# Neighbourhood attention with a mixture of experts on one core: the order of two products, and the layout of the transposed bias rows

## The chip, the cores and the metric

The kernel runs on one core of a Trainium2 chip. The metric is the device time of one execution in microseconds. Before the change it was run three times (median 4380.1 us, 4376.23 to 4390.58). One further execution was recorded by the hardware profiler; all lines of profiles come from such an execution, and line numbers (L445) are those of the kernel.

## The reference

Input x is 2 x 128 x 256 x 256 (batch, channels, rows, columns), all in float32. The output is two residual steps:

```python
x = x + conv(_ln_c(x), W_qkv, W_out, rel_height, rel_width)   # attention
t = _to_tokens(x)
t = t + ffn(_ln_t(t), router_w, router_b, expert_w, expert_b) # top-2 of 8 experts
```

The attention works on windows of 8 x 8 queries and 12 x 12 keys around them, with 4 heads of 32 channels:

```python
q = q * SCALE
attn = jnp.einsum('bnd,bmd->bnm', q, k)
attn = attn + rel_pos_emb(q, rel_height, rel_width) + FIXED_MASK
attn = jax.nn.softmax(attn, axis=-1)
out = jnp.einsum('bnm,bmd->bnd', attn, v)
```

`FIXED_MASK` is minus infinity wherever the row or the column distance is odd in its table, so that a query only meets keys of its own row and column parity. `rel_pos_emb` adds to a score a term that depends on the query and the row distance, and one on the query and the column distance. The second step gives each token to the two experts with the highest router probability, weighted.

## The kernel before, in words

The image is cut into strips of 8 rows, 32 a batch item, 64 in all. Because of the mask, a strip falls apart into four independent planes (two row parities by two column parities), each of 4 x 128 pixels. The main loop (L809) makes one turn for each of the 256 planes, and seven more for what is left of the experts. In one turn, `n`, it does the attention of plane n, the projections of plane n + 1, and one piece of 512 tokens of the normalisation, the routing and the experts of earlier rows. Everything of the loop stands in a section in which the order of each engine's instructions is the order in which the code issues them (L808), so the sequence of generator steps (`next(...)`) in the loop is the schedule. TensorE (PE) makes products, VectorE (DVE), ScalarE (ACT) and GpSimd (POOL) everything between, and all DMAs are issued from the queue of SyncE (SP).

The projections of a plane are in `project` (L400), five steps:

- its first step makes the bias rows `pu` (L408: `wrel` times the plane, 128 x 512, two PE instructions, as any float32 product here), and then calls `value_rows` (L339), in which four products per plane (eight PE instructions of 128 columns) make the value rows `pv`, one for each new row of pixels, and ACT copies them to `vr` (L358);
- the second transposes `pu` in blocks of 32 x 32 on DVE into `uT` (L413);
- the third makes the keys `pk` (L423), which ACT copies into `kcol` (L434, L441);
- the fourth makes the queries `pq` (L445), which ACT copies into `qs` (L447);
- the fifth only stores the names of the tiles.

`pu`, `pv`, `pk`, `pq`, and later in the turn `plt` and `plg` (sums of the normalisation) and `po` (output projection), are all PSUM tiles of one pool, `mm_tile` (L92), with three buffers handed out in turn. So a tile can first be written when the readers of the tile three before it are done.

Between the first and the second step the loop issues `spread` (a transpose of the gates on DVE, L651, and DMAs of it) and `send_values` (L364: the DMA of `vr` to `vrows` in DRAM, from where `take_values`, L374, later fetches the windows). On DVE, the routing of a piece of tokens (`route`, L606, split into three) stands ahead of L651, and so ahead of `uT`.

After the second step the loop calls `shift` (L386): two DVE copies cut the 6 needed distances of rows and of columns out of `uT` into `auT` (L392), and a transpose of `auT` makes `au` (L397), which holds for each pixel's query what is to be added for its row and column distances. Its layout is [partition, 32 m, 4 a, 4 s], where (m, a, s) is the place of a pixel in the plane. The transpose goes through it in the order a, s, m, so that it writes with steps of 16 elements (64 bytes).

In the next turn `scores` (L462) begins with 16 products that spread these terms over the keys, the mask products (L474): 32 PE instructions on tiles of 32 rows and 64 columns of the array, with the constant `keys` as weights and 128 elements of `au` each as the operand that streams through: for 8 values of m (every second one) the 16 values of (a, s), which lie together. Then the scores themselves (L491, 128 instructions) are added into the same PSUM tile `att`, and ACT makes the exponential `pT` (L499). `attend` (L503) makes the sums (L512) and the products with the values (L522), and DVE divides (L532 to L542, among them the transposes `sT` and `rT`).

The experts' products `acc` (L714) come in three groups in a turn, of 8, 6 and 2 instructions of 512 columns: behind `pq`, behind `plt`, and behind `po`. Their operands `xe` are made by DVE (six) and POOL (two) at L705, from gates `gb` that DMAs spread over all partitions; DVE adds `acc` to `xt` at L720.

Of the kernel before, what the change touches and what calls it, by code (L numbers as in the profile page):

```python
# [11 lines left out]
F32 = mybir.dt.float32  # L12
# [5 lines left out]
P = 128  # L18
# [33 lines left out]
def kernel(  # L52
# [16 lines left out]
    nc = tc.nc  # L69
    B, C, H, W = x.shape  # L70
    NS = H // R
    PR, PC = R // 2, W // 2
    NP = PC // 8
# [10 lines left out]
    work = ctx.enter_context(tc.tile_pool(name="work", bufs=2))  # L84
# [7 lines left out]
    def mm_tile(name):  # L92
        return ps_mm.tile([P, 512], F32, tag="mm", name=name)
# [92 lines left out]
    for h in range(HEADS):  # L186
        hp = slice(h * DH, (h + 1) * DH)
# [27 lines left out]
    auT = []  # L215
# [26 lines left out]
    def ln_rows(i):  # L242

        s = strips[i][1]
        return range(1 if s == 0 else 2, KR - 1 if s == NS - 1 else KR)
# [9 lines left out]
    def place(i, k):  # L255

        return (PR * strips[i][1] + k) % KR

    def runs(i, rows):

        out = []
        for k in rows:
            if out and place(i, k) == out[-1][1] + out[-1][2]:
                out[-1][2] += 1
            else:
                out.append([k, place(i, k), 1])
        return out
# [71 lines left out]
    def value_rows(n):  # L339

        i, pl = divmod(n, 4)
        xp = xn[i % 2][:, pl // 2, pl % 2]
        rows, sent = list(ln_rows(i)), []
        for part in (rows[-4:], rows[:-4]):
            if not part:
                continue
            pv = mm_tile(f"pv{n}_{part[0]}")
            m = len(part)
            for j, k in enumerate(part):
                nc.tensor.matmul(  # L350
                    pv[:, j * P : (j + 1) * P],
                    lhsT=xp[:, k, 1 : PC + 1],
                    rhs=wv,
                    start=True,
                    stop=True,
                )
            vr = work.tile([P, 4, P], F32, tag="vr", name=f"vr{n}_{part[0]}")
            nc.scalar.copy(  # L358
                vr[:, 0:m].rearrange("p r c -> p (r c)"), pv[:, : m * P]
            )  # L360
            sent.append((part, vr))
        return sent
# [23 lines left out]
    def shift(uT, n, state):  # L386

        for j in range(2):
            shifted = uT[:, :, :, NU * j + 3 : NU * j + 9]
            dims = [list(d) for d in shifted.ap]  # L390
            dims[1 + j][0] -= 1
            nc.vector.tensor_copy(  # L392
                auT[n % 2][:, :, :, 6 * j : 6 * j + 6],
                bass.AP(shifted.tensor, shifted.offset, dims),
            )
        au = work.tile([P, 2 * NP, PR, 4], F32, tag="au", name=f"au{n}")
        nc.vector.transpose(au.rearrange("p m a s -> p a s m"), auT[n % 2])  # L397
        state["au"] = au

    def project(n, state):  # L400

        i, pl = divmod(n, 4)
        xp = xn[i % 2][:, pl // 2, pl % 2]
        inner = xp[:, 1 : 1 + PR, 1 : PC + 1]
        kk = kcol[pl]

        pu = mm_tile(f"pu{n}")
        nc.tensor.matmul(pu, lhsT=wrel, rhs=inner, start=True, stop=True)  # L408
        state["sent"] = value_rows(n)
        yield  # L410

        uT = work.tile([P, PR, 4, 32], F32, tag="uT", name=f"uT{n}", bufs=1)
        nc.vector.transpose(uT, pu.rearrange("p (a m s) -> p a s m", a=PR, s=4))  # L413
        state["shift"] = lambda: shift(uT, n, state)
        yield

        rows = list(ln_rows(i))
        for part in (rows[-4:], rows[:-4]):
            if not part:
                continue  # L420
            pk = mm_tile(f"pk{n}_{part[0]}")
            m = len(part)
            nc.tensor.matmul(  # L423
                pk[:, : m * PC],
                lhsT=wk,
                rhs=xp[:, part[0] : part[0] + m, 1 : PC + 1],
                start=True,
                stop=True,
            )
            pk3 = pk[:, : m * PC].rearrange("p (r c) -> p r c", r=m)  # L430
            for k, at, m in runs(i, part):
                new = pk3[:, k - part[0] : k - part[0] + m]
                places = kk[:, :, 0:NK].rearrange("p t (c r) -> p t r c", r=KR)[:, :, at : at + m]
                nc.scalar.copy(places[:, 1 : NP - 1], windows(new[:, :, KC - 3 :], 0, NP - 2))  # L434

                ends = [places[:, 0, :, 1:], new[:, :, 0 : KC - 1]]
                for j, step in enumerate(((NP - 1) * SLOT - KR, PC - KC + 1)):
                    dims = [list(d) for d in ends[j].unsqueeze(1).ap]
                    dims[1] = [step, 2]
                    ends[j] = bass.AP(ends[j].tensor, ends[j].offset, dims)  # L440
                nc.scalar.copy(*ends)  # L441
        yield

        pq = mm_tile(f"pq{n}")
        nc.tensor.matmul(pq, lhsT=wq, rhs=inner, start=True, stop=True)  # L445
        qs = work.tile([P, 2 * NP, PR, 4], F32, tag="qs", name=f"qs{n}")
        nc.scalar.copy(  # L447
            qs.rearrange("p m a s -> p a m s"), pq.rearrange("p (a m s) -> p a m s", a=PR, s=4)
        )
        yield  # L450

        state.update(qs=qs, kk=kk, vv=vwin[n % 2])
        yield

    def windows(rows, n0, count):

        first = rows[:, :, 8 * n0 : 8 * n0 + KC].unsqueeze(1)
        dims = [list(d) for d in first.ap]
        dims[1] = [8, count]
        return bass.AP(first.tensor, first.offset, dims)  # L460

    def scores(n, state):  # L462


        qs, kk, au = state["qs"], state["kk"], state["au"]
        turn = place(n // 4, 0) // 2
        att = ps_att.tile([P, 4, 512], F32, tag="att", name=f"att{n}")
        sc = att[:, :, 0:HQ]
        for w in range(2):
            for half in range(2):  # L470
                rows = slice(half * SLOT, (half + 1) * SLOT)
                for h in range(HEADS):
                    hp = slice(h * DH, (h + 1) * DH)
                    nc.tensor.matmul(  # L474
                        sc[rows, h].rearrange("p (t w z) -> p t w z", w=2, z=16)[:, :, w],
                        lhsT=keys[hp, turn, w],
                        rhs=au[hp, half * NP + w : (half + 1) * NP : 2].rearrange(
                            "p t a s -> p t (a s)"
                        ),
                        start=(w == 0),  # L480
                        stop=False,
                    )
        for t in range(HP):
            if t == HP // 2:
                yield
            for half in range(2):
                rows = slice(half * SLOT, (half + 1) * SLOT)
                m0 = 2 * (half * HP + t)
                for h in range(HEADS):
                    hp = slice(h * DH, (h + 1) * DH)  # L490
                    nc.tensor.matmul(  # L491
                        sc[rows, h, 32 * t : 32 * t + 32],
                        lhsT=kk[hp, half * HP + t, :],
                        rhs=qs[hp, m0 : m0 + 2].rearrange("p m a s -> p (m a s)"),
                        start=False,
                        stop=(t == HP - 1),
                    )
        pT = work.tile([P, HEADS, HQ], F32, tag="pT", name=f"pT{n}", bufs=1)
        nc.scalar.activation(pT, att[:, :, 0:HQ], AF.Exp)  # L499
        state.update(att=att, pT=pT)  # L500
        yield
# [276 lines left out]
    for _ in project(0, states[0]):  # L778
        pass
# [28 lines left out]
    with tc.manual_schedule(engines={ET.PE, ET.DVE, ET.Activation, ET.Pool, ET.SP}):  # L808
        for n in range(n_planes + 7):  # L809
            i, pl = divmod(n, 4)  # L810
            score, attn, outp, ahead, norm, rout = none, none, none, none, none, none
            if n < n_planes:
                score = scores(n, states[n])
                attn = attend(n, states[n])
                outp = out_project(n, states[n])
            if n + 1 < n_planes:
                states[n + 1] = {}
                ahead = project(n + 1, states[n + 1])
# [18 lines left out]
            if gated:  # L837
                f, c, made = gated
# [15 lines left out]
            f = (i - 1, pl) if 0 < i <= len(strips) else None  # L854
# [107 lines left out]
```

## Time and profile before

| of the profiled execution | |
|---|---|
| its own time | 4380.58 us |
| span of its instructions | 4378.8 us |
| mean granted TensorE clock | 0.993 |
| PE busy | 4248.2 us |
| PE weight loads busy | 2454.2 us |
| DVE busy | 3853.9 us |
| ACT busy | 1456.6 us |
| POOL busy | 1091.6 us |
| DMA moved | 1022.19 MB, mean 233 GB/s |

Busy time is the sum of the instructions' durations on an engine. In a line of a group of instructions stand the line of the kernel, the engine, the operation, what it writes and reads, the shapes, the count, then the busy time of the group and the mean length of one in ns, and then the time for which the engine was idle just before such an instruction and what ended that wait. PE's weight loads (PEld) are listed apart from its matmuls; they can run beside one another. Matmuls overlap, so their lengths add up to more than the time they take; the distance from start to start is what a sequence of them costs. In a line of waits stand who waited at which line, for whom, the sum in us, how often, and the longest. In the timeline stand the start, the length, the engine, the line and what is written and read; neighbours of one kind are drawn together.

### The profile page before, as it was taken

Reading aid. Unit: us, or ns where it says so; the run is one execution under the profiler, and the core shown is the slowest. Engines: PE = TensorE matmul, PEld = TensorE weight load, DVE = VectorE, ACT = ScalarE, POOL = GpSimd, SP = SyncE. Lnnn points to the kernel's source line nnn. Section 1 sums busy time; section 2 is a strip of 40 time slices with the busy share of each in tenths; the row PEclk is TensorE's granted clock in tenths of the full one; section 3 lists DMA queues with packets and bytes.
Section 4 is the critical chain, followed back from the end, with each engine's and each line's share of the span. In section 5 each row is a group of like instructions: output and inputs, shape, how many; then the busy total and the mean of one; then the engine's idle time right before and its main releaser. Section 6 shows DMA issues by size and latency. Waiting matters only on the chain. (4 is left out here: it accounts for less than half of the span.)

```text
span 4378.8 us, 224652 instructions
## 1 busy us (share of the span) xinstructions
PE 4248.2 (97%) x94273; PEld 2454.2 (56%) x94273; DVE 3853.9 (88%) x11850; ACT 1456.6 (33%) x3774; POOL 1091.6 (25%) x1126
## 2 busy tenths in 40 slices
PE   7899999999999999999999999999999999999987
PEld 5455555555555555555555555555555555555553
DVE  5899889899888989989888889988998888999987
ACT  3333333333333333333333333333333333333321
POOL 1222222222222222222222222222222222222211
PEclk9999999999999999999999999999999999999999
DMA  4677778777777787777777787777777777777766
GB/s 114 210 240 240 244 235 243 241 237 244 233 244 240 244 244 233 243 232 244 238 241 234 240 244 236 243 236 243 238 240 243 236 242 232 244 238 239 243 191 191
DMA packets 824580, 1022.19 MB, mean 233 GB/s; under 512 B 137634, under 2 KB 409634, under 8 KB 823594
## 3 DMA queue, kind: packets, MB, share of 16 engines
q1 hardware_dynamic: 822864, 1007.52, 74.8%
q8 instruction: 769, 12.60, 1.2%
q14 instruction: 217, 1.78, 0.1%
q10 hardware_dynamic: 730, 0.29, 0.0%
HBM read 863.78 MB, written 143.75 MB: 230 GB/s over the span
## 5 line engine op out<-in xcount | busy, mean ns | idle before, releaser
L714 PE MATMUL acc<-xe,ew 128*128 128x512 f32 x4096 | 1916.8, 600 | 21.4 <-DVE gb L688 17.5
L714 PEld LDWEIGHTS acc<-xe,ew 128*128 128x128 f32 x4096 | 757.9, 190 | 941.4 <-issue 872.1
L705 DVE TENSOR_TENSOR xe<-xs,gb 128x512 f32<-128x512 f32 x1536 | 950.5, 686 | 11.8 <-DMA gb<-gd 1.4
L709 POOL COPY last<-xe 128x1 f32<-128x1 f32 x256 | 47.0, 184 | 3088.0 <-DVE gb L688 3081.0
L705 POOL TENSOR_TENSOR xe<-xs,gb 128x512 f32<-128x512 f32 x512 | 650.7, 1272 | 0.7 <-issue 0.5
L276 POOL TENSOR_TENSOR xn<-xt,rb 128x512 f32<-128x512 f32 x249 | 373.7, 1501 | 170.4 <-DMA rb<-gd 164.1
L491 PE MATMUL att<-qs,kcol 32*64 32x32 f32 x32768 | 398.2, 227 | 5.1 <-issue 5.1
L491 PEld LDWEIGHTS att<-qs,kcol 32*64 32x64 f32 x32768 | 395.9, 131 | 6.6 <-issue 6.2
L522 PEld LDWEIGHTS att<-pT,vwin 64*32 64x32 f32 x32768 | 350.2, 105 | 50.4 <-issue 11.8
L522 PE MATMUL att<-pT,vwin 64*32 64x32 f32 x32768 | 350.6, 200 | 8.0 <-issue 6.3
L350 PEld LDWEIGHTS pv<-wt,xn 128*128 128x128 f32 x2048 | 270.1, 192 | 126.5 <-issue 78.7
L434 ACT COPY kcol<-pk 128x560 f32<-128x560 f32 (+2 forms) x344 | 319.0, 927 | 52.8 <-PE pk L423 49.4
L499 ACT ACTIVATE pT<-att 128x1024 f32<-128x1024 f32 x256 | 261.8, 1023 | 208.0 <-PE att L491 207.2
L445 PE MATMUL pq<-xn,wt 128*128 128x512 f32 x512 | 274.7, 617 | 30.0 <-DVE uT L413 26.0
L574 ACT ACTIVATE sq<-xt 128x512 f32<-128x512 f32 x505 | 291.9, 629 | 0.0
L408 PE MATMUL pu<-xn,wrel 128*128 128x512 f32 x512 | 291.7, 651 | 0.0
L397 DVE STREAM_TRANSPOSE au<-auT 128x512 f32<-128x512 f32 x256 | 272.3, 1064 | 9.0
L550 PE MATMUL po<-o,wt 128*128 128x512 f32 x512 | 264.4, 598 | 8.4 <-DVE o L542 5.8
L350 PE MATMUL pv<-wt,xn 128*128 128x128 f32 x2048 | 271.2, 275 | 0.8 <-issue 0.8
L532 DVE STREAM_TRANSPOSE sT<-att 128x512 f32<-128x512 f32 x256 | 183.5, 717 | 98.7 <-PE att L522 84.7
L423 PE MATMUL pk<-xn,wt 128*128 128x512 f32 (+2 forms) x528 | 262.9, 582 | 1.3 <-DVE uT L413 1.3
L474 PEld LDWEIGHTS att<-au,keys 32*64 32x64 f32 x8192 | 117.9, 133 | 227.8 <-PE po L550 183.5
(2696 smaller groups left out, 4895.9 us busy)
## 6 DMA issues: line engine op xcount, KB each, us to landing
gb<-gd SPq DMA_DIRECT2D x2048, 256.0 KB, 5.8
vwin<-vrows SPq DMA_DIRECT2D x512, 240.0 KB, 5.4
xt<-in_x_dram SPq DMA_DIRECT2D x256, 256.0 KB, 6.6
sb<-gd SPq DMA_DIRECT2D x256, 256.0 KB, 4.1
out_dram<-xt SPq DMA_DIRECT2D x256, 256.0 KB, 6.2
rb<-gd SPq DMA_DIRECT2D x249, 256.0 KB, 3.4
vrows<-vr SPq DMA_DIRECT2D x168, 256.0 KB, 3.9
vrows<-vr SPq DMA_DIRECT2D x160, 128.0 KB, 3.5
```

The lines of the kernel that those rows point to most:

```text
L276: eng.tensor_tensor(xn[i % 2][:, :, :, k, 1 : PC + 1], ln1_src(i, k).rearrange("p (y j x) -> p y x j", y=2, x=2), rb.rearrange("p (y j x) ...
L350: nc.tensor.matmul(pv[:, j * P : (j + 1) * P], lhsT=xp[:, k, 1 : PC + 1], rhs=wv, start=True, stop=True,)
L397: nc.vector.transpose(au.rearrange("p m a s -> p a s m"), auT[n % 2])
L408: nc.tensor.matmul(pu, lhsT=wrel, rhs=inner, start=True, stop=True)
L434: nc.scalar.copy(places[:, 1 : NP - 1], windows(new[:, :, KC - 3 :], 0, NP - 2))
L445: nc.tensor.matmul(pq, lhsT=wq, rhs=inner, start=True, stop=True)
L491: nc.tensor.matmul(sc[rows, h, 32 * t : 32 * t + 32], lhsT=kk[hp, half * HP + t, :], rhs=qs[hp, m0 : m0 + 2].rearrange("p m a s -> p (m a ...
L522: nc.tensor.matmul(av[hp, half, 32 * t : 32 * t + 32], lhsT=vv[rows, t, hp], rhs=pT[rows, h, 32 * t : 32 * t + 32], start=True, stop=True,)
L550: nc.tensor.matmul(po, lhsT=wo, rhs=state["o"].rearrange("p f z -> p (f z)"), start=True, stop=True)
L574: nc.scalar.activation(sq, src, AF.Square)
L705: eng.tensor_tensor(self.xe[e], self.xs, self.gb.pop(e), ALU.mult)
L714: nc.tensor.matmul(self.acc, lhsT=ew[:, e, :], rhs=self.xe.pop(e), start=(e == 0), stop=not self.xe)
```

## The change

It has two parts. In the first step of `project`, `value_rows` is called ahead of the bias rows' product, not behind it; the tiles of the pool are so handed out in the order `pv`, `pu`, `pk`, `pq`. And `au` gets the layout [partition, 4 a, 4 s, 32 m]: the transpose at L397 writes it in a row, and the mask products read it through a view in which neighbouring values of (a, s) lie 32 elements (128 bytes) apart, and the m two elements. What is computed is the same.

```diff
@@ in shift
-        au = work.tile([P, 2 * NP, PR, 4], F32, tag="au", name=f"au{n}")
-        nc.vector.transpose(au.rearrange("p m a s -> p a s m"), auT[n % 2])
+        au = work.tile([P, PR, 4, 2 * NP], F32, tag="au", name=f"au{n}")
+        nc.vector.transpose(au, auT[n % 2])
         state["au"] = au
@@ in project
+        state["sent"] = value_rows(n)
         pu = mm_tile(f"pu{n}")
         nc.tensor.matmul(pu, lhsT=wrel, rhs=inner, start=True, stop=True)
-        state["sent"] = value_rows(n)
         yield
@@ in scores
                         lhsT=keys[hp, turn, w],
-                        rhs=au[hp, half * NP + w : (half + 1) * NP : 2].rearrange(
-                            "p t a s -> p t (a s)"
-                        ),
+                        rhs=au[hp].rearrange("p a s m -> p m (a s)")[
+                            :, half * NP + w : (half + 1) * NP : 2
+                        ],
                         start=(w == 0),
```

## The prediction

> **What bounds the kernel now.** I read the busy shares first, then the groups of instructions around the change, then the waits, and last the timeline of one turn (one plane; 256 of them make up nearly all of the span).
>
> ```profile
> PE 4248.2 (97%) x94273; PEld 2454.2 (56%) x94273; DVE 3853.9 (88%) x11850; ACT 1456.6 (33%) x3774; POOL 1091.6 (25%) x1126
> ...
> L445 PE MATMUL pq<-xn,wt 128*128 128x512 f32 x512 | 274.7, 617 | 30.0 <-DVE uT L413 26.0
> ...
> L397 DVE STREAM_TRANSPOSE au<-auT 128x512 f32<-128x512 f32 x256 | 272.3, 1064 | 9.0
> ```
>
> TensorE (PE) is busy almost always and VectorE (DVE) nearly so; ACT and POOL have room. PE's only regular idle time that names another engine stands before the query product pq, and it ends on the transpose uT. The waits say the same more strongly on PE's weight loads, and show that DVE waits for PE too:
>
> ```profile
> PEld pq L445 <- DVE uT L413: 176.7, 235, 2.0
> DVE uT L413 <- PE pu L408: 35.3, 13, 12.3
> DVE sT L532 <- PE att L522: 84.7, 150, 3.7
> ```
>
> The timeline shows one such turn (start, length, engine, line):
>
> ```profile
> 2023.24 1.13 PE L408 MATMUL pu<-xn,wrel 128*128 128x512 f32 x2
> 2024.20 1.05 PE L350 MATMUL pv<-wt,xn 128*128 128x128 f32 x8
> 2025.09 1.02 PE L423 MATMUL pk<-xn,wt 128*128 128x512 f32 x2
> 2025.29 0.59 ACT L358 COPY vr<-pv 128x512 f32<-128x512 f32 x1 [0.93 <-PE pv L350]
> 2025.52 0.67 DVE L413 STREAM_TRANSPOSE uT<-pu 128x512 f32<-128x512 f32 x1
> 2026.24 0.30 PEld L445 LDWEIGHTS pq<-xn,wt 128*128 128x128 f32 x2 [0.96 <-DVE uT L413]
> 2026.24 1.13 PE L445 MATMUL pq<-xn,wt 128*128 128x512 f32 x2
> 2026.59 1.05 DVE L397 STREAM_TRANSPOSE au<-auT 128x512 f32<-128x512 f32 x1
> ```
>
> pq has to wait because the pool of PSUM tiles for these products has three buffers, handed out in order: pu, pv, pk, and pq gets pu's, free only when uT has read it. DVE comes to uT late: it has the routing chain ahead of it.
>
> From the start times, over all turns: a turn is 16.65 us (median 16.52). pk start to pq start is 1.040 us in the mean, 0.861 where nothing holds it; pq start to the next product 0.923 against 0.861 (its weight load is no longer hidden). So the stall is 0.179 + 0.062 = 0.241 us a turn, 62 us in all. PE without it needs 16.65 - 0.24 = 16.41 us a turn (the shortest regular lengths of its stages add up to 16.27). DVE, without its idle time before sT (98.7 us in its group, 0.39 a turn), needs 16.27. The two engines are nearly level, and each waits a little for the other.
>
> [...] pu, first behind the 32-row products, takes 0.966. [...] The contiguous ones agree (rT 711 ns for 512); au, written with steps of 64 bytes, takes 1064, [...]. [...] The trace agrees for writes: au, and kcol (24-byte steps: 1191 ns for 560 elements and 676 for 280, so 1.84 ns an element, against 0.82 for vr at 512 and 128). For reads it shows nothing in SBUF; a read from PSUM with 16-byte steps, uT, is not slowed (677 ns, against 717 for sT read in a row). No row shows TensorE reading with such steps.
>
> **The change, part by part.**
>
> 1. *Value rows first.* The eight pv matmuls (0.888 us) and two of pu (0.966) swap. Nothing is added. The load that is not hidden, 0.105 us (0.966 - 0.861), passes from pu to the first pv: sum zero. The ring of buffers turns: pv takes the one that plt had, free long before; pu the one that held plg, whose last reader is the routing's L621: PE starts pv 1.57 us after that now (0.32 at worst), and pu will stand in the same second place, so nothing is lost. pq now gets pv's, free after the copy vr on ACT. On ACT vr stands behind pT alone, which ran from 2023.35 to 2024.37 in the turn shown; pv would be written by about 2024.4 (0.99 us after 2023.24, and some 0.17 to be seen), and vr takes 0.59, so it is over near 2025.0. A pq that nothing holds starts at 2025.95 (0.86 after pk's 2025.09). The cover is 0.9 us; gone, it would cost what is missing. The stall of 0.241 us goes.
>
> 2. *What is late next.* pu ends 0.89 us later. uT starts 1.90 us after pu in the median and cannot before 1.16: it will meet pu's end with 0.15 us to wait in such a turn. Behind uT on DVE stand auT, au, xs, six xe, the acc addition and then sT. From pu's end PE has pk, pq, eight acc, ones and att, 0.86 + 0.86 + 3.52 + 0.46 + 1.27 = 6.97 us, to att's end; DVE needs from uT to sT 7.0 us now (2008.85 to 2015.86 in the turn before the one shown), so without part 3 this would be a tie.
>
> 3. *au in a row.* DVE: 1064 - 711 (rT, the nearest row) = 353 ns a turn, 90 us of DVE time. It is not taken from the end directly, as PE is the longer: DVE falls to about 15.9 us a turn against PE's 16.41, and reaches sT about 0.35 us ahead of PE. This is the cover that lets part 1's gain stand.
>
> 4. *Mask products read with a stride.* 32 matmuls (eight at a time on the 32x64 tiles: four rounds of 128 columns at 0.833 ns, the rate of acc's 512 in 427, and some 60 ns: 0.487 us from first to next stage). Each element now lies 128 bytes from the one before. This is on PE, ahead of everything, so any price counts whole. From below, nothing: a gain is excluded, since these reads already run at the rate of contiguous ones. From above: the step that writes show, 0.69 ns an element (au, 353/512) to 1.02 (kcol, 1.84 - 0.82), over 4 x 128 elements is 0.35 to 0.52 us a turn, 90 to 134 us. If the rate just halves: 0.427 us, 109 us. I take nothing, because the one strided read by a compute engine here (uT) is free while strided writes are not; both ends stay for the range.
>
> 5. *DMA.* vr is ready up to 0.9 us earlier, but its transfer stands on SP behind that of gT, which does not move. Number, size and order of transfers stay: nothing. The first project, ahead of the loop, and the tail without attention: under 2 us.
>
> **Sum**, against the profiled execution's own 4380.6 us (span 4378.8 and 1.8 around it; the median of the runs is 4380.1, the same): -62 for the stall, +8 held back because DVE's length varies (the end of uT lies 0.74 us after pk's start in the median, 1.46 in one turn of ten, which eats into later margins), 0 for the stride: 4380.6 - 54 = **4327 us**.
>
> **Rivals.** *Half rate (ends slower).* The mask reads [...] run at half the rate: 0.487 becomes 0.914. PE is the bound, so 4380.6 - 54 + 109 = 4436, with the prices of writes 4417 to 4461. For it: [...] the prices of au and kcol. Against it: uT. It decides from 0.21 us a turn: a round of 160 ns in place of 107, 1.25 ns an element in place of 0.83. *A part of it.* Half that price, +54: 4381, no change. *PE waits elsewhere.* The stall at pq goes but returns before po (which waits for o) or before acc (which waits for its addition), as DVE is held by other things: its L235 rows go up to over a microsecond now and then, [...]. Against it: po follows o by about 1 us now and DVE gets 0.35 shorter. Then some 20 us remain: 4360.
>
> **How the numbers follow.** Stride free 0.48; half rate 0.36; a part 0.11; waits elsewhere 0.05. A measurement can tell about 0.3%, 13 us, from no change. Faster: the first and the last, and 0.01 of the part: 0.54. Within: 0.07 of the part. Slower: half rate and 0.03: 0.39. The likeliest alone gives 4310 to 4345; with both signs in play the range goes from 4308 to 4442, which leaves out a little of the first case and two fifths of the half rate.
>
> **What would show it.** pk to pq at 0.86 in nearly every turn, and the waits of pq for uT gone; pq's tile free by vr. au near 711 ns. DVE waiting longer before sT, and a short wait of uT for pu in many turns. The number that decides is the mask stage, first mask matmul to first score matmul: 0.49 if reads are free, 0.91 at half rate, and the mean of the mask matmul (284 ns now) with it. Wrong would be: that mean near 400, or a new wait before po or acc of over 0.1 us a turn.

## The result, and the profile after

The changed kernel is slower. Its median is 4401.64 us (four runs, 4399.92 to 4407.06) against 4379.5 us of four runs of the kernel before, a ratio of 1.0048 with a 95% interval of 1.0028 to 1.0068. In a later comparison it was 1.0036 (1.0024 to 1.0047). The forecast was 4327 us and faster; the rival of half rate named the right side, at 4436. The time lies inside the stated range, but that range took in both signs. The profiled execution has a span of 4405.3 us against 4378.8, so 26.5 us more.

The mask products of the kernel before, from its groups:

```profile
L474 PE MATMUL att<-au,keys 32*64 32x128 f32 x8192 | 180.6, 284 | 31.2 <-issue 31.2
```

From the page of the changed kernel, the busy shares and two groups of instructions:

```profile
PE 4317.1 (98%) x94273; PEld 2555.3 (58%) x94273; DVE 3762.1 (85%) x11850; ACT 1453.1 (33%) x3774; POOL 1088.3 (25%) x1126
...
L474 PE MATMUL att<-au,keys 32*64 32x128 f32 x8192 | 285.5, 396 | 31.2 <-issue 31.1
...
L445 PE MATMUL pq<-xn,wt 128*128 128x512 f32 x512 | 261.8, 592 | 0.8 <-issue 0.8
```

From its groups with shapes kept apart, the transpose:

```profile
L397 DVE STREAM_TRANSPOSE au<-auT 128x512 f32<-128x512 f32 x256 | 182.1, 711 | 9.0
```

DVE is 92 us shorter, and the wait of pq for uT is gone (0.8 us of idle time in place of 30.0). PE is 69 us longer: a mask matmul takes 396 ns on average, not 284. The waits of the changed kernel say where the rest of the slack went:

```profile
DVE uT L413 <- PE pu L409: 188.3, 245, 15.1
...
PEld pq L445 <- issue: 115.5, 480, 0.3
...
DVE sT L532 <- PE att L522: 70.0, 245, 1.9
```

DVE now waits for pu in nearly every turn (245 times). The roles have changed: at pq PE no longer waits for DVE, and DVE waits for PE. (15.1 us of the 188.3 are one wait at the start.) A turn of the changed kernel in the timeline:

```profile
2020.49 1.11 PE L474 MATMUL att<-au,keys 32*64 32x128 f32 x32
...
2022.86 1.16 PE L350 MATMUL pv<-wt,xn 128*128 128x128 f32 x8
...
2023.86 1.02 PE L409 MATMUL pu<-xn,wrel 128*128 128x512 f32 x2
2024.06 0.59 ACT L358 COPY vr<-pv 128x512 f32<-128x512 f32 x1
...
2024.72 1.02 PE L423 MATMUL pk<-xn,wt 128*128 128x512 f32 x2
2024.92 0.72 DVE L413 STREAM_TRANSPOSE uT<-pu 128x512 f32<-128x512 f32 x1 [0.65 <-PE pu L409]
...
2025.58 1.02 PE L445 MATMUL pq<-xn,wt 128*128 128x512 f32 x2
```

pk to pq is 0.86 us, and vr has read pv's tile by 2024.65, 0.93 us ahead of pq. From the start times over all turns: a turn takes 16.759 us in the mean, against 16.654, and its median, quartiles and tenth percentile are all 16.69, which fits a turn whose length PE alone sets. Of the 0.105 us between the means, the mask stage (first mask matmul to first score matmul) gives +0.400 (0.496 to 0.896), the stall at pq -0.241 to nothing, and late starts at three fixed instructions of a turn -0.081 (they are explained below). These make +0.078; the other 0.027, some 7 us in all, is spread over other stages (0.015 of it lies in pv and pu together) and was not traced to a cause.

### The profile page after: what moved, and what is told of

Its sections match the earlier page's. It is cut to its first block, busy times and chain, and to the rows that moved or that the text cites. A ratio compares the mean times of both kernels' runs of the same rounds, so it can differ in the third digit from the quotient of the medians.

```text
span 4405.3 us, 224653 instructions
## 1 busy us (share of the span) xinstructions
PE 4317.1 (98%) x94273; PEld 2555.3 (58%) x94273; DVE 3762.1 (85%) x11850; ACT 1453.1 (33%) x3774; POOL 1088.3 (25%) x1126
## 5 line engine op out<-in xcount | busy, mean ns | idle before, releaser
L491 PEld LDWEIGHTS att<-qs,kcol 32*64 32x64 f32 x32768 | 423.4, 133 | 15.1 <-issue 6.0
L413 DVE STREAM_TRANSPOSE uT<-pu 128x512 f32<-128x512 f32 x256 | 183.4, 716 | 188.5 <-PE pu L409 188.3
L474 PE MATMUL att<-au,keys 32*64 32x128 f32 x8192 | 285.5, 396 | 31.2 <-issue 31.1
L350 PE MATMUL pv<-wt,xn 128*128 128x128 f32 x2048 | 303.1, 292 | 0.3 <-issue 0.3
L474 PEld LDWEIGHTS att<-au,keys 32*64 32x64 f32 x8192 | 160.1, 140 | 236.0 <-PE po L550 183.7
L409 PE MATMUL pu<-xn,wrel 128*128 128x512 f32 x512 | 266.0, 601 | 0.0
L445 PE MATMUL pq<-xn,wt 128*128 128x512 f32 x512 | 261.8, 592 | 0.8 <-issue 0.8
L350 PEld LDWEIGHTS pv<-wt,xn 128*128 128x128 f32 x2048 | 253.5, 194 | 11.2 <-issue 0.7
```

Of the source, the lines that this page charges most:

```text
L350: nc.tensor.matmul(pv[:, j * P : (j + 1) * P], lhsT=xp[:, k, 1 : PC + 1], rhs=wv, start=True, stop=True,)
L474: nc.tensor.matmul(sc[rows, h].rearrange("p (t w z) -> p t w z", w=2, z=16)[:, :, w], lhsT=keys[hp, turn, w], rhs=au[hp].rearrange("p a s ...
L491: nc.tensor.matmul(sc[rows, h, 32 * t : 32 * t + 32], lhsT=kk[hp, half * HP + t, :], rhs=qs[hp, m0 : m0 + 2].rearrange("p m a s -> p (m a ...
```

## The experiments

All ratios are against runs of the kernel before on the same chip. In the table, the three columns of times are means per turn in us, worked out from the start times of PE's instructions: the mask stage; the stall at pq (pk to pq above 0.861 and pq to acc above 0.861); the late starts at the three fixed places (starts over 60 ns later than the median of that place, summed and divided by 256). Each row of these columns comes from one profiled execution. "No stride, other elements" is the whole change with mask products that read a row of other elements.

| kernel | ratio (95%) | mask stage | stall at pq | fixed places |
|---|---|---|---|---|
| before | 1 | 0.496 | 0.241 | 0.127 |
| the change | 1.0048 (1.0028 to 1.0068) | 0.896 | 0 | 0.046 |
| part one alone | 0.9863 (0.9847 to 0.9879) | 0.489 | 0 | 0.137 |
| part two alone | 1.0133 (1.0117 to 1.0149) | 0.896 | 0.149 | 0.094 |
| runs of two | 0.9855 (0.9836 to 0.9873) | 0.509 | 0 | 0.124 |
| no stride, other elements | 0.9872 (0.985 to 0.9895) | 0.493 | 0 | 0.157 |
| order as before, u in PSUM | 0.9914 (0.989 to 0.9938) | 0.496 | 0.025 | 0.285 |

### One part at a time

Part one alone is the kernel before with this edit:

```diff
+        state["sent"] = value_rows(n)
         pu = mm_tile(f"pu{n}")
         nc.tensor.matmul(pu, lhsT=wrel, rhs=inner, start=True, stop=True)
-        state["sent"] = value_rows(n)
```

> Part one alone: value rows ahead of the bias rows, au written and read as in the kernel before. Theory (the change lost by its strided reads alone, 0.40 us a turn, and its first part gained): the mask stage stays at 0.49 us, pk to pq falls from 1.04 to about 0.86, and the time is 4320 to 4345 us, ratio 0.987 to 0.992; DVE, not shortened, is then about as long as PE and some of its lateness shows before po or acc. Rival (the first part gains nothing without the shorter transpose, because DVE is the next bound): within 0.3% of the kernel before, 4367 to 4393 us.

It came out 1.4% faster, 4334.5 us against 4395.9 of the kernel before beside it: the theory's side, with a ratio just below its 0.987. From the waits of this kernel:

```profile
DVE uT L413 <- PE pu L409: 71.5, 47, 14.5
...
DVE sT L532 <- PE att L522: 14.6, 20, 1.6
```

DVE waits for att only 20 times, where it was 150 before: it is about as long as PE now, as the forecast's part 2 had it, but that tie costs little. The lateness that the theory looked for shows neither before po nor before acc; it shows before the next turn's first mask product, which starts over 60 ns late in 65 turns in place of 11: 0.042 us a turn, 11 us. What ends that wait the profile does not name. The median turn is 16.32 us, next to the 16.27 of PE's shortest stages.

Part two alone is the other half of the change (the layout of au and the view in `scores`), with the order as before.

> Part two alone: au written in a row and read with steps of 128 bytes, the order of the two products as before. Theory: the mask stage is 0.90 us, and as PE is 0.40 us longer and DVE 0.35 us shorter, uT is nearly always in time for pq: pk to pq about 0.86 to 0.88 without the first part. The turn is set by PE at about 16.7 to 16.75 us and the time is that of the whole change, 4395 to 4412 us. Rival (the parts add up, the stall at pq of 0.24 us stays): 4400 + 62, about 4460 us.

Neither was right. It is 1.3% slower, 4452.5 us against 4395.9 (the rival's 4460, beside the 4380 of the first comparison, is a ratio of 1.018); that is not the whole change's time, and not the full price of the stride either, which is 0.40 us in each of 256 turns, 102 us or 2.3%. From its waits:

```profile
DVE sT L532 <- PE att L522: 212.5, 254, 4.0
PEld pq L445 <- DVE uT L413: 128.6, 238, 2.1
```

DVE has time to spare (it waits 212.5 us for att), and yet PE's weight loads wait 128.6 us for uT. So it is not the mean length of DVE's work that makes uT late. What does is shown by the experiment with u further down.

The whole change was run again beside the kernel before, on the chip on which the two parts had been run:

> The whole change once more, beside the kernel before on the chip of the other runs of this call. Theory: ratio 1.003 to 1.007 as on record, the mask stage 0.896 us and pk to pq 0.86. Rival (the chips differ in what the change does): below 1.000, as the product of the two parts' ratios (0.9863 x 1.0133 = 0.9994) would have it.

It came to 1.0036, with a mask stage of 0.896 us, no stall at pq and 0.040 us at the fixed places, by the theory; the product of the parts' ratios, 0.9994, is not what the whole does. By the table, part two leaves 0.149 us of the stall for part one to take, not 0.241; and part one leaves 0.137 us at the fixed places, which fall to 0.046 with the stride.

### The stride taken away, in two ways

Runs of two keep the same work with another layout; each pair of values lies together, so that the transpose writes every second element and the mask products read two elements, then jump 256 bytes:

```diff
-        au = work.tile([P, PR, 4, 2 * NP], F32, tag="au", name=f"au{n}")
-        nc.vector.transpose(au, auT[n % 2])
+        au = work.tile([P, 2 * PR, 2 * NP, 2], F32, tag="au", name=f"au{n}")
+        nc.vector.transpose(
+            au.rearrange("p g m z -> p g z m"),
+            auT[n % 2].rearrange("p a (q z) m -> p (a q) z m", z=2),
+        )
...
-                        rhs=au[hp].rearrange("p a s m -> p m (a s)")[
+                        rhs=au[hp].rearrange("p g m z -> p m g z")[
```

> The whole change with another layout of au, [8, 32 m, 2]: the transpose writes with steps of 8 bytes and the mask products read runs of two elements (8 bytes) 256 bytes apart, [...]. Theory [...]: transpose about 711 ns, mask stage 0.49 us, time 4300 to 4335 us, faster than both. Rival one (any break in a run costs): mask stage about 0.69 us or more, 4350 us or more. Rival two (reads are fine, writes with steps are not): transpose near 1064 ns, mask stage 0.49, time as with part one alone.

From its groups:

```profile
L477 PE MATMUL att<-au,keys 32*64 32x128 f32 x8192 | 183.2, 283 | 31.3 <-issue 31.2
L397 DVE STREAM_TRANSPOSE au<-auT 128x512 f32<-128x512 f32 x256 | 182.4, 713 | 9.0
```

Both sides are at the price of elements in a row: 713 ns for the transpose, 283 for a mask matmul (0.509 us for the stage, 0.02 above the row of 16). It beats both kernels, 4330.4 us against 4395.9 before. It does not clearly beat part one alone: the intervals overlap, though DVE is 0.35 us a turn shorter. So theory on both prices, and on the time no more than part one alone.

The second way keeps the layout of the change and reads other elements:

> The whole change, but the mask products read 16 elements in a row in place of 16 elements 128 bytes apart (they then add bias terms of other pixels: the bias is not that of the reference). It is the change without the price of the stride. Theory: mask stage 0.49 us, a turn of 16.28 to 16.35 us set by PE, 4290 to 4320 us. Rival (something else in the change costs as well, such as the order of loads on PE): 4340 us or more.

This one reads in a row and gives 0.9872, again the ratio of part one. The mask stage is as the theory had it (0.493); the time, 4334 us, lies between the theory's 4290 to 4320 and the rival's 4340, on a chip where the kernel before took 4396. With the stride gone, what is left of the change is worth part one and nothing more that these runs can tell, and the fixed places keep 0.157 us.

### What a step costs, and on which engine

In these kernels the mask products read au with another inner step, `[[..], [t, 8], [k, 16]]` with k of 2 or 4 elements (t of 32 or 64), in place of 32.

> The whole change, but the mask products read au with steps of 8 bytes in place of 128 (they add bias terms of other pixels: the bias is not that of the reference). Theory [...]: mask stage 0.49 to 0.51 us. Rival (a price by the length of the step, or for any step): 0.6 us or more.

> The same with steps of 16 bytes. Theory ([...] at half rate): mask stage 0.90 us, as with 128 bytes. Rival (a price that grows with the step, [...]): clearly below 0.90.

From the groups of the kernel with steps of 8 bytes, and then of that with 16:

```profile
L474 PE MATMUL att<-au,keys 32*64 32x128 f32 x8192 | 185.8, 287 | 31.5 <-issue 31.5
```

```profile
L474 PE MATMUL att<-au,keys 32*64 32x128 f32 x8192 | 295.2, 406 | 31.4 <-issue 31.4
```

The stage is 0.521 us at 8 bytes (a little above the theory's 0.51), 0.930 at 16, 0.896 at 128. So the price is there at 16 bytes and nearly gone at 8, and it is no higher at 128 than at 16. Why steps of 8 bytes are nearly free and those of 16 are not, these runs do not show. By the medians of the stage, 0.487 and 0.896, the price at 128 bytes is 0.409 us over 512 elements, 0.80 ns each, close to the 0.83 of half rate.

Is it a matter of eight small tiles that read at once? Here, in part one alone, `po` reads `o` with steps of 128 bytes:

```diff
-            po, lhsT=wo, rhs=state["o"].rearrange("p f z -> p (f z)"), start=True, stop=True
+            po, lhsT=wo, rhs=state["o"].rearrange("p f (b a) -> p a f b", a=32), start=True, stop=True
```

> Part one alone (au as in the kernel before), but the output product po, all 128 rows and two instructions of 512 columns, reads o with steps of 128 bytes in place of elements in a row (its columns then belong to other pixels: the output projection is added at other places). Theory (the price belongs to each element [...], 0.83 ns, whatever the tile): po's stage goes from 0.858 to 1.71 us. Rival (it belongs to the eight small tiles that read at once): po's stage stays near 0.86.

From the groups of part one alone, and then of this kernel:

```profile
L550 PE MATMUL po<-o,wt 128*128 128x512 f32 x512 | 264.2, 598 | 9.4 <-DVE o L542 5.8 <-DVE gb L688 3.6
```

```profile
L550 PE MATMUL po<-o,wt 128*128 128x512 f32 x512 | 482.8, 1031 | 9.4 <-DVE o L542 5.8 <-DVE gb L688 3.6
```

The stage went from 0.858 to 1.707 us (medians), 0.83 ns an element, with the whole array and one product at a time. And other engines' reads:

```diff
-        nc.vector.tensor_tensor(o, av[:, 0:2], rT, ALU.mult)
+        nc.vector.tensor_tensor(
+            o.rearrange("p f (k b) -> p f k b", b=8),
+            av[:, 0:2].rearrange("p f (k b) -> p f k b", b=8),
+            rT.rearrange("p f (b k) -> p f k b", b=8),
+            ALU.mult,
+        )
...
-            nc.scalar.activation(sq, src, AF.Square)
+            nc.scalar.activation(
+                sq.rearrange("p (k b) -> p k b", b=16), src.rearrange("p (b k) -> p k b", b=16), AF.Square
+            )
```

> Part one alone, and two reads from SBUF with steps of 128 and 64 bytes where elements in a row stood: rT by DVE at line 542 of the kernel before, steps of 32 elements (o then holds products with other pixels' sums), and the square of x by ACT at line 574, steps of 16 elements and written in a row (the squares are then summed with other pixels). It shows whether reads with steps cost other engines too. Theory [...]: about 0.7 to 1 ns more an element, line 542 from 691 to 1040 ns or more, line 574 from 629 to 1000 ns or more. Rival (it is TensorE's own): 691 and 629 within 30 ns.

Both reads in fact step by 128 bytes (32 elements): in the square too, where the expectation has 16 elements. From the groups of part one alone, and then of this kernel:

```profile
L574 ACT ACTIVATE sq<-xt 128x512 f32<-128x512 f32 x505 | 292.4, 630 | 0.0
...
L542 DVE TENSOR_TENSOR o<-att,rT 128x512 f32<-128x512 f32 x256 | 177.0, 692 | 8.9
```

```profile
L579 ACT ACTIVATE sq<-xt 128x512 f32<-128x512 f32 x505 | 536.7, 1115 | 0.0
...
L542 DVE TENSOR_TENSOR o<-att,rT 128x512 f32<-128x512 f32 x256 | 271.6, 1061 | 8.9
```

692 became 1061 ns on DVE and 630 became 1115 on ACT: 0.72 and 0.95 ns an element. Reads from SBUF with steps of 128 bytes cost 0.72 to 0.95 ns an element on the three engines tried, about what the writes of au and kcol cost (0.69 and 1.02).

### Why uT is late

In the kernel before, the lateness of uT goes with two small operations of the normalisation. DVE's L235 and L238 need 0.17 us, and often take more. From the timeline of a turn of the kernel before:

```profile
2001.34 1.49 POOL L276 TENSOR_TENSOR xn<-xt,rb 128x512 f32<-128x512 f32 x1 [1.85 <-DMA rb<-gd]
...
2002.17 0.68 DVE L235 SCALAR_TENSOR_TENSOR u__118_37817<-u__118_37817,epsc 128x8 f32<-128x8 f32 x1
...
2002.79 1.27 POOL L705 TENSOR_TENSOR xe<-xs,gb 128x512 f32<-128x512 f32 x1
...
2003.37 0.71 DVE L238 SCALAR_TENSOR_TENSOR u__118_37817<-u__118_37817,r__118_37818 128x8 f32<-128x8 f32 x1 [0.52 <-ACT r__118_37818 L237]
```

L235 ends at 2002.85 and POOL's instruction at 2002.83; L238 at 2004.08 and POOL's at 2004.06. Over the trace, 126 of 260 L235 took more than 0.3 us; every one of these started while a POOL instruction ran and ended about 0.02 us behind that instruction's end. The excess of the two over 0.17 us and the wait of pq in the same turn have a correlation of 0.95: in turns with under 0.1 us of excess the wait is 0.01 us or less, in those with over 0.8 it is about 0.8. Two neighbours of the same size behave otherwise: L233 and L234, which take one input from plg in PSUM, needed 165 ns at most, and began and ended inside one POOL instruction 231 and 221 times of 260; L235, with both inputs in SBUF, never did. That the place of the inputs makes the difference was the author's guess. So one of them was taken out of SBUF:

```diff
-        u, r = (
+        u0, r = (
             small.tile([P, 2, NT], F32, tag=v, name=f"{v}_{name}")[:, k0:k1] for v in ("u", "r")
         )
+        u = free[:, 0 : (k1 - k0) * NT].rearrange("p (k t) -> p k t", t=NT)
...
-        nc.vector.tensor_tensor(u, r, mean, ALU.mult)
-        nc.vector.scalar_tensor_tensor(u, u, -1.0, sq, ALU.mult, ALU.add)
+        nc.vector.tensor_tensor(u0, r, mean, ALU.mult)
+        nc.vector.scalar_tensor_tensor(u, u0, -1.0, sq, ALU.mult, ALU.add)
...
-        r, u = rstd(p4, k0, k1, nm)
+        r, u = rstd(p4, k0, k1, nm, plg[:, P : 2 * P])
```

> The kernel before, order and au as they were, but the small tile u of the normalisation lies in unused columns of the PSUM tile plg, so that the DVE operations at lines 235, 238 and 239 of the kernel before read one operand from SBUF, not two. Theory (uT is late because those operations now and then run for 0.4 to 1.2 us in place of 0.17, until an operation on POOL ends, and this spread is what pq waits for): they take 0.2 us each time, pk to pq falls from 1.04 to 0.90 us or less without a change of order, and the time is 0.7 to 1.3% less than before, 4325 to 4350 us of 4380. Rival (uT is late because the chain from sT to uT is too long in any case): pk to pq stays over 1.00, the time within 0.3%.

```profile
L236 DVE SCALAR_TENSOR_TENSOR plg<-plg,epsc 128x8 f32<-128x8 f32 x245 | 42.5, 173 | 8.4
```

That operation (now line 236) takes 173 ns in the mean and 175 at most, pk to pq is 0.870 us, and the stall is down to 0.025 us a turn without any change of order. So the cause of nearly all of the stall is this spread, and part one helps because pq's tile no longer hangs on uT. The time fell by 0.9%, not by the 1.4% of part one. In the profiled execution the fixed places took more, 0.285 us a turn in place of 0.127; but it was the slowest of four (4346 to 4369 us), so how much of the difference they make up in general is not shown.

### The fixed places

The kernel aligns PE's instructions at the head of each turn (`addr_align`, with `BLOCK, FIRST_LIMIT = 256, 99`): a border between blocks of 256 instructions falls 99 instructions after the turn's first. With 99, late starts that no other engine explains come at the same three instructions: the 18th score matmul, the 4th acc matmul of the group of eight, the 108th value matmul. They are 256 instructions apart (128 matmuls, each with its weight load). The DMA queue for instructions brings 769 packets of 16 KB, three a turn. In the traces a late start lies 1.4 us behind the end of such a packet, at each of the three places (in this order 1.36, 1.47 and 1.41 us in the median before; 1.48, 1.41 and 1.40 with u in PSUM). Two kernels with au in runs of two move the boundaries:

```diff
-BLOCK, FIRST_LIMIT = 256, 99
+BLOCK, FIRST_LIMIT = 256, 93
```

> The change with au in runs of two, and the constant that places a turn's first instructions in a block of 256 set from 99 to 93, six instructions (three matmuls) earlier. Theory (what PE still loses at three fixed instructions of a turn is the wait for the next block of 256 instructions, worst where a block is used up in 3.7 us): the late starts move from the 18th to the 15th score matmul, from the 4th acc matmul to the boundary between pq and acc, and from the 108th value matmul to the 105th; the shortest block lasts 4.9 us in place of 3.7, the late time behind it falls, and the time is 0.2 to 0.8% below that of the runs of two with 99 (ratio 0.977 to 0.984). Rival (these waits are for data): the late starts stay at the same matmuls and the time is the same, ratio 0.984 to 0.988.

The places moved by three matmuls, as they must if they belong to blocks; the time went the wrong way, to 1.0052 (1.0033 to 1.0072), against 0.9855 with 99. From the group of acc with 99 (runs of two), and then with 93:

```profile
L717 PE MATMUL acc<-xe,ew 128*128 128x512 f32 x4096 | 1914.2, 600 | 19.6 <-DVE gb L691 15.4 <-issue 2.4 <-DVE xt L723 1.7
```

```profile
L717 PE MATMUL acc<-xe,ew 128*128 128x512 f32 x4096 | 1915.9, 601 | 70.8 <-issue 51.6 <-DVE gb L691 15.8 <-DVE xt L723 1.6
```

The boundary between pq and acc now comes 5.1 us after the boundary before it. Its packet ends, in the median, 3.7 us after that earlier boundary; with 1.4 us more that makes 5.1, and no room is left. Half the turns (133 of 249) wait there by more than 60 ns, 0.29 us in the mean, 74 us in all. The shortest block with 99 waited less; its packet starts early (about 0.6 us after the boundary before, in the median, against 2.7 for this one).

> The change with au in runs of two and the constant of a turn's placement 97 in place of 99, one matmul earlier. With 93, one boundary between blocks of 256 instructions fell at the first acc matmul, 5.1 us after the one before it, and half the turns waited there. Theory (a block is ready 1.4 us after its packet lands, about 3.8 us after the boundary before, so 5.7 us are enough in most turns): late starts at the 17th score, the 3rd acc and the 107th value matmul, ratio 0.983 to 0.992. Rival (any boundary off the one with 99 costs as 93 did): over 0.997.

With 97 the places moved by one and the ratio is 0.991 (0.989 to 0.993), in the range of the theory, and still behind 99. So these waits move with the blocks and follow the packets. That PE waits for its instructions there is the author's reading; the profile names nothing that ends these waits. Between kernels whose PE work differs by some tenths of a microsecond a turn they differ by up to 0.24 us a turn (0.046 to 0.285), one execution of each. What sets a packet's time was not tested, and why the changed kernel waits less here (0.046, and 0.040 when run again) was not settled.

## Why the prediction was wrong

**Part 4, the stride: the step that failed.** "I take nothing, because the one strided read by a compute engine here (uT) is free while strided writes are not". uT reads PSUM, and the reads from SBUF with steps of 128 bytes paid about as the writes did: 0.80 to 0.83 ns an element on TensorE, 0.72 on DVE, 0.95 on ACT. The upper side of the bound, the prices of au and kcol (0.69 to 1.02 ns), held the truth: 0.400 us a turn, 102 us, 0.78 ns an element. The price of half rate, 0.427, was within 7%. The prediction's own sign of being wrong, a mean near 400 ns, came: 396. It had seen the price coming and given it 0.36; what failed is the reason for taking nothing, a read from PSUM used as evidence on reads from SBUF.

**Part 1, the order.** Right: the stall of 0.241 us went, pq takes pv's tile, vr is out of the way with 0.9 us to spare, the hidden and unhidden load change places (pv's stage goes from 0.888 to 0.995 us, pu's from 0.966 to 0.864, in the median). Alone it is worth 1.4%, about 60 us; the sum had -62, and held 8 of them back for lateness that would show elsewhere. In the changed kernel no lateness showed elsewhere; in part one alone 11 us did, before the mask products.

**Part 3, the shorter transpose.** 353 ns were foreseen and 353 came (1064 to 711). "This is the cover that lets part 1's gain stand" was wrong: part one alone, without it, is as fast as the kernel with runs of two, as far as these runs can tell. With the two engines level, what DVE's extra length may have cost is the 11 us before the mask products, which is within the spread of the runs; the profile does not name what ends that wait.

**Part 2, uT meets pu.** It does, and more than the 0.15 us foreseen: 188 us over the run, some 0.7 a turn. The stride, which makes PE the longer, is a part of that: with runs of two the wait is 103 us (172 times).

**Part 5, DMA, at nothing.** Missing from the list were the late starts at the fixed places. They shrank from 0.127 to 0.046 us a turn, 21 us, a gain that the sum had not. The half-rate rival's 4436 us, with the reserve of 8 taken back, the price at 102 and not 109, and these 21 us, is 4436 - 8 - 7 - 21 = 4400. The median measured is 4401.6, but these terms come from the profiled execution, which took 4407: there 7 us stay open, so the close match to the median is in part luck.

The rival *a part of it* was wrong as well in its reason (the price is whole); its time, 4381, was the nearest of the four, by luck. *PE waits elsewhere* did not happen.

## What to carry to other kernels

Before a stride is moved from one engine's write to another's read, price it on both sides and ask which engine has room. Here, in float32, reads from SBUF with steps of 128 bytes cost 0.72 to 0.95 ns an element on three engines, and writes 0.69 with steps of 64 bytes (au, DVE) and 1.02 with 24 (kcol, ACT); a layout in runs of two elements made both sides nearly free (713 ns for the transpose, 283 for a mask matmul). The read from PSUM that cost nothing (uT, 677 ns with steps of 16 bytes) was no evidence on the reads from SBUF. Where an engine waits on a tile's reader, the order in which buffers are handed out can cure it without making anything shorter, as it did here (0.241 us a turn to nothing), and the wait may come from the spread of a small operation (L235, 0.16 to 1.25 us), not from the mean.

## What the runs showed that was not expected

- The float32 operand au, which TensorE streams from SBUF, ran at nearly half rate with steps of 16 and of 128 bytes (0.930 and 0.896 us for a stage of 0.487), and at almost full rate with steps of 8 (0.521).
- DVE's L235 and L238, of 8 elements with both inputs in SBUF, took 0.16 to 1.28 us in the kernel before, the long ones up to the end of a POOL operation; L235 with one input in PSUM took 0.17 (175 ns at most).
- PE's late starts at the ends of blocks of 256 instructions lay 1.36 to 1.48 us behind the packet's end, in the median of each place. Six instructions of placement moved the time by 2% (1.0052 and 0.9855, each against the kernel before on its own chip).
